# The first image's sampling table, written in whole 2 KB entries from tiles that hold four rows of a column

## The chip, the cores and the metric

The kernel runs on one core of a Trainium2 chip. The metric is the device time of one execution in microseconds (us); for a set of runs the median is given. A core has five engines that run their own instruction streams: PE (TensorE, matrix products and transposes), DVE (VectorE), ACT (ScalarE), POOL (GpSimd) and SP (SyncE, which in this kernel only issues DMAs). [...] A packet is one contiguous run that one DMA engine moves. PE writes its results to PSUM, and DVE or ACT copy them on.

## The reference

The input x is four images of 256 channels and 64 x 64 positions, in float32. Layer 0 adds to x a modulated deformable convolution of the group-normalised image (32 groups): a 3x3 convolution gives, for each position and each of nine taps, an offset in y, an offset in x and a mask; each tap samples the normalised image bilinearly at its displaced position (zero outside the image), is multiplied by the mask, and the nine samples are contracted with w_conv.

```python
om = conv(gn(x), w_off) + b_off                       # 27 channels: 18 offsets, 9 masks
ys = off[:, :, 0] + hs + ki ;  xs = off[:, :, 1] + ws + kj
sampled = bilinear(gn(x), ys, xs) * sigmoid(mask)     # four neighbours with weights
x = x + einsum('bckhw,ock->bohw', sampled, w_conv)
```

Layer 1 treats the 4096 positions of an image as tokens: a layer norm, an attention over the four images with eight heads, a second layer norm, and a mixture of eight experts of which each token takes two. Nothing of layer 1 is touched here.

## The kernel before

**The table.** Bilinear sampling is done by fetching rows. For each image the kernel writes a table to HBM (`tables[b]`, line 327) of 66 x 67 entries, one for each position with a border. An entry is 2 KB: the 256 channels of the position one row above (the half `two=0`), and then the 256 channels of the position itself (`two=1`). Entry (y, x) thus holds the image's rows y-1 and y, counted from zero, at column x-1. One indirect DMA on POOL (line 748, `gather`) then fetches for 128 positions and one tap two adjacent entries, 4 KB in a row, which are the four neighbours. There are 1152 gathers, 288 for an image.

**The first image.** Images 1 to 3 are prepared among the sampling steps of the image before them; image 0 has nothing to hide under, and its preparation is the head of the kernel:

1. SP loads image 0 (4 MB) in four pieces of 1 MB: a half of the channels, and a half of the 4096 positions each (`load_piece`, lines 360 to 370). Behind them on SP's queue come w_off in two DMAs (line 376), b_off (382), w_conv in two of 1.1 MB (394) and the router (168).
2. SP writes the zero borders of the table (`borders`, lines 404 to 408; five DMAs of 64 to 260 KB). The one of line 406 writes the 134 half entries of the table's last row.
3. DVE takes the group statistics: sixteen `bn_stats` of 512 positions (line 446), each as soon as its piece is there, then a short chain over PE and POOL.
4. In eight blocks of eight image rows, DVE normalises (line 508), PE transposes 128 positions at a time (`turn`, line 517), and ACT and DVE copy the result to a tile `zt` (`leave`, line 530), in which a partition holds one position at a time. For image 0 the eight tiles `zt` are the buffers `gs[0..7]`, into which the gathers will write later. With two rows of 64 positions to a transpose, partitions 0 to 63 of `zt` hold the even rows of the block and partitions 64 to 127 the odd ones, four of them behind each other.
5. After each block SP stores it to the table with four DMAs (line 536): one for each half of the partitions (`yl`) and each half of the entry (`two`). Each moves 256 KB from 64 partitions, in 256 packets of 1 KB, to every second row of the table.
6. PE, ACT and DVE compute offsets, indices and weights of the first two blocks (`offsets`, `positions`). Then the sampling steps start: the gathers, four weighted sums of corners (ACT line 765, DVE line 774), a transpose, and the products with w_conv.

**What sets the order.** For image 0 the order on DVE, ACT and PE is written out: the list `first`, sorted by numbers of steps, is emitted as it stands (lines 711 to 725). The order on SP is the framework's, and it is that of the program. The framework also gives the DMAs of SP's queue eight completion semaphores in turn, and the compiled instruction list shows each DMA waiting until the one eight places before it on the queue has landed. The first gather (line 748) waits for all DMAs that write the table and for the indices of block 0; the gathers then wait for free buffers.

Of the kernel before, what the change touches and what calls it, by code (L numbers as in the profile page):

```python
# [18 lines left out]
B, C, H, W = 4, 256, 64, 64  # L19
HW = H * W  # L20
NCH = C // P
# [6 lines left out]
TH, TW = H + 2, W + 3  # L28
# [9 lines left out]
RB = BLK // W  # L38
# [64 lines left out]
def conv_attn_moe_kernel(  # L103
# [22 lines left out]
    nc = tc.nc  # L126
# [200 lines left out]
    tables = [dram.tile([TH * TW, 2 * C], F32, name=f"table{b}") for b in range(B)]  # L327
# [5 lines left out]
    with ExitStack() as actx:  # L333
# [23 lines left out]
        def image_tile(b):  # L357
            xraw[b] = axs[b % 2].tile([P, NCH, HW], F32, name=f"xraw{b}", tag="xraw")

        def load_piece(b, n):  # L360
            ch, h = divmod(n, 2)
            cols = slice(h * HW // 2, (h + 1) * HW // 2)
            return nc.sync.dma_start(
                xraw[b][:, ch, cols],
                x[b, ch * P : (ch + 1) * P].rearrange("p h w -> p (h w)")[:, cols],
            )

        image_tile(0)
        for n in range(2 * NCH):
            load_piece(0, n)  # L370


        woff_sb = aw.tile([P, NCH, 3, 3, QUAD], F32, name="woff_sb")
# [10 lines left out]
        for kj in range(3):  # L384
            ps = slice(kj * QUAD, (kj + 1) * QUAD)
# [11 lines left out]

        zeros = aw.tile([P, C], F32, name="zeros")
        G.memset(zeros, 0.0)

        def borders(b):
            tv = tables[b].rearrange("(y x) (two c) -> y x two c", x=TW, two=2)
# [15 lines left out]
        for half in range(2):  # L418
            ps = slice(half * 64, half * 64 + 64)
# [9 lines left out]
        params, stores = {}, {}  # L429

        def pieces(b):
# [31 lines left out]
            n = FIRST  # L463
            out_ = later if b else first
            for ch in range(NCH):
                for j in range(NBLK):
                    at = LOADS[2 * ch + 2 * j // NBLK] + LANDED + j % (NBLK // 2)
# [13 lines left out]
            tv = tables[b].rearrange("(y x) (two c) -> y x two c", x=TW, two=2)  # L481
            oms = []

            def block(q, at, table=True, offsets=True, alone=False):

                out_ = [] if alone else later
                y0 = q * RB - 1
                lo, hi = max(y0, 0), min(y0 + RB + 2, H)
                if not offsets:
                    lo, hi = y0 + 1, y0 + RB + 1  # L490
                t = {}
                between = "" if table else "_"

                def norm(ch):
                    if ch == 0:
                        t["xs"] = apad.tile(
                            [P, NCH, RB + 2, W], F32, name=f"xs{b}_{q}{between}",
                            tag="xs" if table or alone else "xs_",
                            bufs=2 if table or alone else 1,
                        )  # L500
                        if offsets and lo > y0:
                            G.memset(t["xs"][:, :, 0, :], 0.0)
                        if offsets and hi < y0 + RB + 2:
                            G.memset(t["xs"][:, :, RB + 1, :], 0.0)
                    to, of = t["xs"][:, ch, lo - y0 : hi - y0], xrv[:, ch, lo:hi]
                    scale, bias = rs[:, ch : ch + 1], nb[:, ch : ch + 1]
                    if alone:
                        V.tensor_scalar(to, of, scale, bias, ALU.mult, ALU.add)
                    else:
                        S.activation(to, of, AF.Identity, bias=bias, scale=scale)  # L510


                def turn(i):
                    xc = t["xs"][:, :, 1 : RB + 1].rearrange("p ch y x -> p ch (y x)")
                    t["tp"] = ps_tp.tile([P, C], F32, name=f"tpx{b}_{q}_{i}", tag="tp")
                    for ch in range(NCH):
                        T.transpose(
                            t["tp"][:, ch * P : (ch + 1) * P], xc[:, ch, i * P : (i + 1) * P],
                            ident,
                        )  # L520

                def leave(i):
                    if i == 0:

                        t["zt"] = (
                            gs[q].rearrange("p (t c) -> p t c", c=C) if alone
                            else azt.tile([P, NT, C], F32, name=f"zt{b}_{q}", tag="zt")
                        )
                    zt = t["zt"]
                    (V.tensor_copy if alone and i == NT - 1 else S.copy)(zt[:, i, :], t["tp"])  # L530
                    if i < NT - 1:
                        return
                    for yl in range(2):
                        for two in range(2):
                            yy = q * RB + yl + 1 - two
                            stores[b] = nc.sync.dma_start(
                                tv[yy : yy + RB - 1 : 2, 1 : W + 1, two, :].rearrange(
                                    "t x c -> x t c"
                                ),
                                zt[yl * W : (yl + 1) * W],  # L540
                            )


                def rows_of(n):
                    if n == 0:
                        t["po"] = ps_om.tile([3 * QUAD, RB, W], F32, name=f"po{b}_{q}", tag="om")
                    ch, ki = divmod(n, 3)
                    T.matmul(
                        t["po"], woff_sb[:, ch, ki].rearrange("p kj o -> p (kj o)"),
                        t["xs"][:, ch, ki : ki + RB],  # L550
                        start=(n == 0), stop=(n == NCH * 3 - 1),
                    )

                oc = ocs[q % 2 if table else 2]

                def shifted(kj):
                    ps = slice(kj * QUAD, (kj + 1) * QUAD)
                    to = slice(max(0, 1 - kj), W - max(0, kj - 1))
                    of = slice(max(0, kj - 1), W - max(0, 1 - kj))
                    S.activation(  # L560
                        oc[ps, :, to], t["po"][ps, :, of], AF.Identity, bias=boff_sb[ps]
                    )

                def summed(half):
                    if half == 0:
                        t["pt"] = ps_om.tile([P, NT, NOFF], F32, name=f"pt{b}_{q}", tag="om")
                    ocf = oc.rearrange("p y x -> p (y x)")
                    for i in range(half * 2, half * 2 + 2):
                        T.matmul(
                            t["pt"][:, i, :], ocf[:, i * P : (i + 1) * P], tap_sum,  # L570
                            start=True, stop=True,
                        )

                def kept():
                    if b and not q:
                        oms.append(atmp.tile([P, NR, NOFF], F32, name=f"om{b}", tag="om"))
                    of[q] = oms[0][:, rows_in(q), :] if b else atmp.tile(
                        [P, NT, NOFF], F32, name=f"om{b}_{q}", tag="om_", bufs=2
                    )
                    V.tensor_copy(of[q], t["pt"])  # L580

                out_.append((at, lambda: norm(0)))
                out_.append((at + 1, lambda: norm(1)))
                if alone and table:
                    for i in range(NT):
                        out_.append((at + 10 + 2 * i, lambda i=i: turn(i)))
                        out_.append((at + 11 + 2 * i, lambda i=i: leave(i)))
                elif table:
                    for i in range(NT):
                        out_.append((at + 3 + 4 * i, lambda i=i: turn(i)))  # L590
                        out_.append((at + 4 + 4 * i, lambda i=i: leave(i)))
                if offsets:
                    for m in range(NCH * 3):
                        out_.append((at + 4 + 2 * m + m // 2, lambda m=m: rows_of(m)))
                    for kj in range(3):
                        out_.append((at + 18 + kj, lambda kj=kj: shifted(kj)))
                    out_.append((at + 22, lambda: summed(0)))
                    out_.append((at + 23, lambda: summed(1)))
                    out_.append((at + 24, kept))
                return out_  # L600

            of = {}

            def rows_in(q):
                return slice(q * NT, (q + 1) * NT)
# [85 lines left out]
            if b:  # L691
# [5 lines left out]
                half = NR // 2  # L697
# [13 lines left out]
            for q in range(NBLK):  # L711
                first.extend(block(q, n + 10 * q, offsets=False, alone=True))
            n += 10 * NBLK + 8
            for q in range(EARLY):
                at = n + 20 * q
                first.extend(block(q, at, table=False, alone=True))
                first.extend(positions(rows_in(q), lambda q=q: of[q], at + 25, 4))
            for q in range(EARLY, NBLK):
                at = (q - 2) * NT * K2 + 12
# [234 lines left out]
        with tc.manual_schedule(engines=order):  # L954
# [7 lines left out]
            for n in range(total + TAP + OUT + 3 * NT):  # L962
                b, at = divmod(n, STEPS)
# [43 lines left out]
    for b in range(B):  # L1007
        for j in range(NBLK):
            if j < HB:
                n = j * B + b  # L1010
# [38 lines left out]
    with ExitStack() as bctx:  # L1049
# [130 lines left out]
        rows = NCH * B  # L1180
# [972 lines left out]
```

## Time and profile before

| what | value |
|---|---|
| median of four runs | 3334.86 us (3330.86 to 3343.88) |
| the profiled execution's own time | 3316.29 us |
| its span, from the first to the last instruction | 3314.5 us |
| busy share of PE, DVE, ACT, POOL | 88%, 74%, 57%, 53% |
| bytes moved, mean rate | 913.00 MB, 275 GB/s |
| table stores of image 0 (line 536) | 32 DMAs of 256 KB, issued from 24.0 to 58.6 us |
| first gather starts | 63.59 us |

The profile is of one execution. Its times count from the first instruction; its own time is 1.8 us longer than its span, which lies around the instructions. A group of instructions is named by its line in the kernel, its engine, the operation, and what it writes from what it reads. On SP's queue the length shown for a DMA is the time for which the queue was occupied with issuing it, waiting included, and not the time of the transfer. The waits name the last thing an instruction waited for, as far as the profile can tell.

### The profile page before, as it was taken

What the parts mean: (1) busy time and instruction counts of PE and PEld (TensorE: products, weight loads), DVE (VectorE), ACT (ScalarE), POOL (GpSimd) and SP (SyncE); (2) the same over time, 40 slices, a digit from 0 to 9 for tenths busy, and PEclk for the clock granted to TensorE, in tenths of its full rate; (3) what the DMA queues carried; (4) which work ended last, traced back from release to release, by engine and by line L of the source; (5) the groups of instructions that cost most, each with busy time, mean ns of one, the idle gap of its engine ahead of it and who ended that gap; (6) DMA issues with size and microseconds to landing.
All of it is one profiled execution on the core that took longest, in us unless ns stands there. A gap on an engine that the chain in (4) does not pass through costs nothing. (4 is left out here: it accounts for less than half of the span.)

```text
span 3314.5 us, 45522 instructions
## 1 busy us (share of the span) xinstructions
PE 2911.6 (88%) x11356; PEld 1700.2 (51%) x11356; DVE 2465.4 (74%) x6413; ACT 1887.0 (57%) x4462; POOL 1749.6 (53%) x1809
## 2 busy tenths in 40 slices
PE   4899998898988899988999999997768788889997
PEld 2445544354444444434444444554434477778885
DVE  5878888987878978888889877885546574434776
ACT  2557665565655566645666656756534455546675
POOL 2555566665656655556666633215553466564442
PEclk7999999999999999999999999998888899999998
DMA  8999999999999999999999969614334445545988
GB/s 270 368 320 351 336 368 368 393 362 341 379 356 370 371 351 353 368 336 378 358 356 362 353 163 177 119 56 145 122 129 136 131 141 163 165 134 173 337 289 274
DMA packets 348547, 913.00 MB, mean 275 GB/s; under 512 B 42566, under 2 KB 125821, under 8 KB 345984
## 3 DMA queue, kind: packets, MB, share of 16 engines
q0 software_dynamic: 208368, 689.10, 58.2%
q1 hardware_dynamic: 129488, 197.93, 19.4%
q10 hardware_dynamic: 10432, 23.07, 1.8%
q8 instruction: 95, 1.56, 0.2%
q14 instruction: 164, 1.34, 0.1%
HBM read 741.09 MB, written 171.60 MB: 275 GB/s over the span
## 5 line engine op out<-in xcount | busy, mean ns | idle before, releaser
L748 POOL DMA_INDIRECT g<-table,idx x1152 | 1107.0, 961 | 765.5 <-DVE s L774 383.2
L808 PE MATMUL acc<-sT,wconv_sb 128*128 128x512 f32 x2304 | 1221.9, 613 | 26.1 <-ACT sT L796 11.1
L774 DVE SCALAR_TENSOR_TENSOR partial<-g,wts,s 128x256 f32<-128x256 f32 x1152 | 565.5, 491 | 233.2 <-ACT s L765 114.0
L765 ACT ACTIVATE s<-g,wts 128x256 f32<-128x256 f32 x1152 | 589.2, 511 | 196.1 <-DMA g<-table,idx 110.9
L788 PEld LDWEIGHTS tps<-ident,s 128*128 128x128 f32 x2304 | 304.5, 149 | 718.9 <-issue 481.1
L796 ACT COPY sT<-tps 128x256 f32<-128x256 f32 x1152 | 422.1, 366 | 401.3 <-PE tps L788 134.1
L788 PE MATMUL tps<-ident,s 128*128 128x128 f32 x2304 | 467.7, 286 | 141.6 <-issue 57.0
L774 DVE SCALAR_TENSOR_TENSOR s<-g,wts,s 128x256 f32<-128x256 f32 x1152 | 551.2, 478 | 0.0
L774 DVE SCALAR_TENSOR_TENSOR s<-g,wts,partial 128x256 f32<-128x256 f32 x1152 | 546.4, 474 | 0.7
L1935 POOL DMA_INDIRECT ys_rows<-y,to x277 | 275.5, 995 | 289.8 <-DVE y L1930 215.1
L808 PEld LDWEIGHTS acc<-sT,wconv_sb 128*128 128x128 f32 x2304 | 358.9, 196 | 38.6 <-issue 15.4
L1907 PE MATMUL ph<-xT,w 128*128 128x256 f32 (+1 forms) x1288 | 281.6, 362 | 52.3 <-ACT hT L1911 26.7
L1508 POOL DMA_INDIRECT xs_rows<-u,slots x256 | 248.3, 970 | 114.9 <-issue 69.0
L1930 DVE TENSOR_TENSOR y<-py,w 128x512 f32<-128x512 f32 (+1 forms) x161 | 99.3, 617 | 238.8 <-PE py L1925 76.6
L1925 PE MATMUL py<-w,hT 128*128 128x256 f32 x1108 | 273.2, 387 | 0.6 <-ACT w L1874 0.6
L1907 PEld LDWEIGHTS ph<-xT,w 128*128 128x128 f32 x1288 | 215.3, 195 | 82.5 <-ACT hT L1911 36.5
L1911 ACT ACTIVATE hT<-ph,w 128x256 f32<-128x256 f32 (+1 forms) x322 | 134.9, 443 | 198.3 <-PE ph L1907 95.7
L1925 PEld LDWEIGHTS py<-w,hT 128*128 128x128 f32 x1108 | 212.4, 195 | 30.0 <-ACT w L1874 1.0
L1290 DVE SCALAR_TENSOR_TENSOR mix<-pv,att,mix 128x512 f32<-128x512 f32 x192 | 132.8, 743 | 88.4 <-remote 78.1
L1325 PE MATMUL po<-wo_sb,mix 128*128 128x265 f32 x512 | 135.2, 419 | 37.3 <-DVE mix L1314 36.0
L322 DVE SCALAR_TENSOR_TENSOR junk<-q,k 128x512 f32<-128x512 f32 x224 | 141.5, 686 | 21.0 <-ACT k L1107 21.0
L1299 ACT ACTIVATE gate<-pg,bg_c 128x512 f32<-128x512 f32 x60 | 40.2, 683 | 202.4 <-DVE mix L1314 129.7
(291 smaller groups left out, 3599.1 us busy)
## 6 DMA issues: line engine op xcount, KB each, us to landing
xt<-xs_rows SPq DMA_DIRECT2D x116, 260.0 KB
yk<-ys_rows SPq DMA_DIRECT2D x56, 512.0 KB
table<-zt SPq DMA_DIRECT2D x96, 256.0 KB
g<-table,idx POOLq DMA_INDIRECT x1152
t<-o SPq DMA_DIRECT2D x32, 530.0 KB
t<-bo_sb POOLq DMA_DIRECT2D x32, 530.0 KB
dt<-t SPq DMA_DIRECT2D x64, 265.0 KB
xraw<-in_x SPq DMA_DIRECT2D x16, 1024.0 KB
```

What stands on the lines that cost most here:

```text
L322: V.scalar_tensor_tensor(junk, qks[s_, j, ch][0], 1.0, qks[t_, j, ch][1], ALU.mult, ALU.mult, accum_out=parts[:, ch, s_ * B + t_, j : j + 1],)
L748: g = G.indirect_dma_start(out=gs[n % NGB], out_offset=None, in_=tables[b], in_offset=bass.IndirectOffsetOnAxis(ap=params[b][0][:, r, k : ...
L765: first = S.activation(ss[n], gs[n % NGB][:, :C], AF.Copy, scale=params[b][1][:, 0, r, k : k + 1])
L774: last_corner[n] = V.scalar_tensor_tensor(kept if c == 1 else ss[n], gs[n % NGB][:, c * C : (c + 1) * C], params[b][1][:, c, r, k : k + 1] ...
L788: T.transpose(tps[n][:, ch * P : (ch + 1) * P], s[:, ch * P : (ch + 1) * P], ident)
L796: S.copy(sTs[tap][:, :, i * P : (i + 1) * P], tps.pop(n).rearrange("p (ch t) -> p ch t", ch=NCH),)
L808: T.matmul(accs[block, oh], wconv_sb[:, ch, k, oh * P : (oh + 1) * P], sTs[tap][:, ch, :], start=(k == 0 and ch == 0), stop=(k == K2 - 1 a ...
L1325: T.matmul(po[:, n, :CR], o[:, ch, i * P : (i + 1) * P], wo_sb[:, ch, :], start=(ch == 0), stop=(ch == NCH - 1),)
L1508: s = G.indirect_dma_start(out=rows_, out_offset=bass.IndirectOffsetOnAxis(ap=slots[:, k, n : n + 1], axis=0), in_=u[:, n % NT, :], in_off ...
L1907: T.matmul(ph, w1_sb[:, ch, f * P : (f + 1) * P], xT[:, ch, :], start=(ch == 0), stop=(ch == NCH - 1),)
L1925: T.matmul(py[:, i, :], hT[:, f, i * P : (i + 1) * P], w2_sb[:, f, :], start=(f == 0), stop=(f == NCH - 1),)
L1935: s = G.indirect_dma_start(out=ys_rows[g], out_offset=bass.IndirectOffsetOnAxis(ap=to[:, i : i + 1], axis=0), in_=y[:, i, :], in_offset=No ...
```

## The change

Two things change, both for image 0 only. The line numbers of the changed kernel are up to 24 higher from there on.

First, image 0 is loaded in eight pieces of 512 KB (a half of the channels, a quarter of the positions) where there were four of 1 MB.

Second, the rows of a block are dealt out otherwise, and the table is stored otherwise. DVE's normalisation writes the eight rows in the order 0, 4, 1, 5, 2, 6, 3, 7, by an access pattern alone, so that the transposes put rows 0 to 3 of the block on partitions 0 to 63 and rows 4 to 7 on partitions 64 to 127. A partition of `zt` then holds four consecutive rows of one column, one behind the other, and two neighbouring kilobytes in it are a whole table entry. `leave_whole` stores each half of the partitions with three DMAs: three whole entries of each column (192 packets of 2 KB, read from overlapping windows of the tile, 384 KB), the first half of the entry behind them and the second half of the entry ahead of them (64 packets of 1 KB each, 64 KB). That is six DMAs for a block where there were four, 48 where there were 32, and the same 8 MB.

```diff
-        def load_piece(b, n):
-            ch, h = divmod(n, 2)
-            cols = slice(h * HW // 2, (h + 1) * HW // 2)
+        def load_piece(b, n, each=2):
+            ch, h = divmod(n, each)
+            cols = slice(h * HW // each, (h + 1) * HW // each)
...
-        for n in range(2 * NCH):
-            load_piece(0, n)
+        for n in range(4 * NCH):
+            load_piece(0, n, 4)
...
+        def overlapping(rows, n):
+
+            at = rows.ap
+            return bass.AP(rows.tensor, rows.offset, [at[0], [C, n], [1, 2 * C]])
...
                     if alone:
+                        if table:
+
+                            to = to.rearrange("p (m h) w -> p m h w", h=2)
+                            of = of.rearrange("p (h m) w -> p m h w", h=2)
                         V.tensor_scalar(to, of, scale, bias, ALU.mult, ALU.add)
...
                     if i < NT - 1:
                         return
+                    if alone:
+                        leave_whole(zt)
+                        return
...
+                def leave_whole(zt):
+
+                    half = RB // 2
+                    th = tables[b].rearrange("(y x) e -> x y e", x=TW)
+                    for h in range(2):
+                        ps, r = slice(h * W, (h + 1) * W), q * RB + h * half
+                        nc.sync.dma_start(
+                            th[1 : W + 1, r + 1 : r + half], overlapping(zt[ps], half - 1)
+                        )
+                        nc.sync.dma_start(tv[r + half, 1 : W + 1, 0], zt[ps, half - 1])
+                        stores[b] = nc.sync.dma_start(tv[r, 1 : W + 1, 1], zt[ps, 0])
```

The four stores of a block (line 536) stay for images 1 to 3, and so do their loads in four pieces.

## The prediction

> **What bounds the kernel now.** The change touches the first 64 us, so I read the profile from there. First, busy times by stretch (columns: stretch, length, busy us of PE, PEld, DVE, ACT and POOL, PE's granted clock, share and rate of the DMA engines):
>
> ```profile
> 0.00:24.00 24.00, 3.87 (x16) 3.37 (x16) 16.49 (x39) 2.44 (x5) 7.18 (x21) 1.00 0.85 297
> 24.00:62.00 38.00, 23.74 (x94) 12.78 (x92) 16.02 (x57) 12.64 (x30) 0.21 (x1) 0.83 0.87 230
> 62.00:68.00 6.00, 0.00 (x0) 0.00 (x0) 0.00 (x0) 0.05 (x1) 3.50 (x4) 0.50 0.49 116
> 68.00:168.00 100.00, 80.34 (x273) 38.39 (x274) 88.15 (x220) 53.84 (x130) 62.41 (x66) 0.87 0.98 372
> ```
>
> The head has two halves. To 24 us the DMA engines load and DVE computes statistics; from 24 to 62 us they are 87% busy, at only 230 GB/s, while every compute engine is mostly idle. From 68 us on they are 98% busy with gathers, so what the head loses nothing wins back, and what it saves moves the end one for one.
>
> Second, the timeline of SP's queue, and of the engines it serves (columns: start, us, engine, line, what):
>
> ```profile
> 16.34 0.80 SPq L406 DMA_DIRECT2D table<-zeros  x1
> 17.19 5.15 SPq L407 DMA_DIRECT2D table<-zeros  x1
> 22.38 0.79 SPq L408 DMA_DIRECT2D table<-zeros  x1
> 24.03 35.64 SPq L536 DMA_DIRECT2D table<-g  x32
> ```
>
> ```profile
> 33.22 0.42 DVE L530 COPY g<-tpx 128x256 f32<-128x256 f32 x1 [0.99 <-PE tpx L517]
> ...
> 56.43 0.19 DVE L643 TENSOR_TENSOR wts<-lo 128x36 f32<-128x36 f32 x1
> ```
>
> ```profile
> 63.59 1.24 POOL L748 DMA_INDIRECT g<-table,idx  x1 [31.55 <-DMA bo_c<-in_bo]
> ...
> 67.95 0.51 ACT L765 ACTIVATE s<-g,wts 128x256 f32<-128x256 f32 x1 [13.97 <-DMA g<-table,idx]
> 68.49 0.49 DVE L774 SCALAR_TENSOR_TENSOR partial<-g,wts,s 128x256 f32<-128x256 f32 x1 [11.86 <-ACT s L765]
> ```
>
> DVE normalises from 20.68 us, the first tile is complete at 23.96, the last at 33.64, and the last weights of the two prepared blocks at 56.6. The 32 stores occupy SP from 24.03 to 59.67, 1.11 us each. The completion events of the trace put the last landing at 62.6 (2.9 us after its issue ended), POOL starts the first gather 0.95 later, and its data reach ACT at 67.95 and DVE at 68.49. So the table's stores end last; the compute chain has 68.49 - 56.62 = 11.9 us to spare.
>
> Third, what a store costs SP (columns: ns least/median/most), and what the DMA engines reach from 26 to 61 us (the stores) and from 3304 to 3306 us (output, 2 KB packets from 128 partitions):
>
> ```profile
> L536 SPq DMA_DIRECT2D table<-g x32: 574/1132/1893, 24.0 to 58.6; - x32
> ...
> L404 SPq DMA_DIRECT2D table<-zeros x4: 677/786/1216, 14.8 to 1391.1; - x4
> ...
> L405 SPq DMA_DIRECT2D table<-zeros x4: 595/646/730, 15.7 to 1391.8; - x4
> ...
> L2023 ACTq DMA_DIRECT2D out<-oT x27: 383/384/452, 3062.3 to 3288.4; - x27
> ```
>
> ```profile
> DMA packets 8450, 8.17 MB, mean 233 GB/s; under 512 B 496, under 2 KB 8448, under 8 KB 8448
> ...
> DMA packets 375, 0.74 MB, mean 368 GB/s; under 512 B 18, under 2 KB 18, under 8 KB 375
> ```
>
> SP is held back while it issues the stores: an unhindered one takes 0.57, the median 1.13. The limit is behind it, at 233 GB/s. The packet records say more: between 26 and 61 us half of the 1 KB packets took 44 to 48 ns and three in eight 65 to 85, with little between, while of the 1 KB packets from 200 to 1700 us, spread between gathers, 96% took 46 or 47. A 1 KB packet is not slow in itself; something is shared in the head that is shared by bytes. What the head has and those have not is sixteen DMA engines reading the same 64 partitions at once.
>
> **The change part by part.**
>
> *Image in eight pieces.* The first `bn_stats` starts at 5.99, when 1 MB has landed. At 424 GB/s (the same view for 4 to 12 us) 512 KB less is 1.2 us. DVE then runs gapless to 17.25 (16 statistics of 0.61 us and 1.5 us of small work), and later pieces come every 1.24 us for 1.22 us of work, so the first tile is complete at about 22.8. But SP issues the last border (line 408) until 23.2, because line 407 was held 5.15 us: the 134 rows of line 406 go through one DMA engine (one completion event, at 27.8). That does not move, so the first store starts at about 23.4: -0.6 us. The four further issues (0.4 us each) push w_off on SP from 3.0 to about 4.6 us; and since the pieces now take all eight completion semaphores, w_off and w_conv each wait for a piece of the image. Their packets stand behind the image anyway: w_off landed at 15.2 and is read at 34.2, w_conv at 21.7, read at 80.8. Cost nothing; without that cover, 1.6 us.
>
> *Row order.* Sixteen DVE instructions of 0.49 us with another pattern, runs of 64 elements. Bounds: nothing, or 0.04 each (the 0.53 of the 576-element form), 0.6 us, under the stores, as tiles are complete 26 us before the last store. Nothing.
>
> *Stores, DMA side.* The 8.39 MB stay. If bytes over shared partitions are the limit, 8.39 MB / 233 GB/s = 36.0 us, as before, 2.23 us for each of sixteen half blocks (35.64 / 16). If packets were the limit, the nearest row is the output, 368 GB/s: 22.8 us, 1.43 each. That row has 2 KB packets and also 128 partitions; the stores get only the first. The two heaps decide: I take 2.23.
>
> [...]
>
> *Stores, SP side.* A half block was two issues and is now three. The whole one (192 packets) is nearest to the unhindered line 536, 0.60. The small one has its twins in lines 404 and 405, the same shape into the same table: 0.60 to 0.85 in the head; I take 0.62. With 0.05 between issues: 0.60 + 2 x 0.62 + 0.15 = 1.99 us, 31.8 for sixteen. Bounds: 0.38 for a small one (the output's issue) gives 1.49 and 23.8 us; 0.79 (median of line 404) gives 2.36 with 0.63 for the whole, 37.8 us.
>
> *Semaphores.* A DMA waits for the one eight places ahead. That was 2 MB of stores and is 1.33 MB, 5.7 us of work against 2.9 us from issue to landing: enough. The sixth store still waits for line 406 (27.8); it would be ready at 26.5. Until then five stores with 0.98 MB are out, 4.2 us of transfer from 24 on: the engines do not run dry. Behind a blocked SP stand only further stores, and the small vectors of line 157 that come in 60 us too early.
>
> *Sum.* The half block costs the larger of 2.23 (DMA) and 1.99 (SP). Start -0.6; the stretch 0, or -1 where SP's deeper queue lets the two partition halves overlap more; I take -1. First gather at 62.0 instead of 63.59: **-1.6 us**, from 3316.3 to 3314.7 for the profiled execution. The median shown lies 18.6 us above that, so 3333.3. Outer bounds: with 1.49 for a half block the stores are done before the weights, which come 1.2 us earlier too, and the spare ends at 12 to 13 us: -12.6. With 2.36, 37.8 - 35.6 - 0.6 = +1.6.
>
> **The rivals.**
>
> *A, SP becomes the bound at 1.99.* If 2 KB packets pass faster, the stores take 31.8 instead of 35.64, start 0.6 earlier, and the last small one lands some 1.7 us sooner after its issue: -6 us, 3329. For it: 84 ns for a 2 KB packet in the output. Against it: the two heaps. Still within 0.3%.
>
> *B, both limits give way.* Small issues at 0.38 and packets at the output's rate: -10 to -12.6 us, 3322 to 3325. Against it: no 64-row store of this trace was issued in under 0.57.
>
> *C, slower: SP's issue takes the place of the transfer.* 48 issues instead of 32, at the place where SP stands before every store. It decides once a small store takes over 0.74 us (0.60 + 2 x 0.74 + 0.15 = 2.23). One of the two twins in the head took 0.85: 2.45 each, 39.2 us, +3 us after the earlier start, 3338. For it: the median of line 404. Against it: line 405 in the same place, 0.60.
>
> *D, no change at all,* since the border of line 406 and the bytes both stay: 0, 3335.
>
> **How the numbers follow.** Forecast (0 to -3 us) 0.5, A 0.2, B 0.08, C 0.12, D 0.1. A measurement of this kernel tells some 0.3% (10 us) from no change; the four runs shown span 13 us. Only B crosses that line by itself, and a noisy comparison adds a few in a hundred on either side: faster 0.11, same 0.82, slower 0.07. The range takes in B's near end at the bottom (3325) and C with the runs' spread at the top (3341).
>
> **What would show it.** Right: line 536's successors occupy SP until 57 to 59 us at about 230 to 245 GB/s, whole stores held above 0.6 us; the first gather at 61 to 63; `bn_stats` from 4.8 us with no earlier first store to match than 23.2. Wrong: first gather before 56, rate over 300 GB/s in the stretch (2 KB packets did pass faster, or both halves of the partitions are read together); or small stores of 0.8 us and a gather after 64; or a difference that arises behind 68 us.

## The result, and the profile after

The changed kernel takes 3342.89 us (median of 52 runs, 3330.09 to 3360.09), the kernel before 3331.03 us (78 runs, 3311.17 to 3345.80). The ratio is **1.0037, 95% interval [1.0028, 1.0046]**: slower by 12 us, with an interval of 9.3 to 15.3 us. The prediction was 1.6 us less than before, 3333.3 us in a range of 3324 to 3341. It started from the median of the four runs shown to it, 3334.86, which lies 3.8 us above that of all 78.

The profiled execution of the changed kernel took 3353.99 us (span 3352.2). Its timeline, SP's queue from the last borders to the fourth store, then two half blocks of the steady part (start, us, engine, line; line 561 is the whole store of 384 KB, 564 and 565 the two small ones of 64 KB):

```profile
17.84 5.47 SPq L412 DMA_DIRECT2D table<-zeros  x1
23.37 0.38 SPq L413 DMA_DIRECT2D table<-zeros  x1
23.86 0.88 SPq L561 DMA_DIRECT2D table<-g  x1
24.78 1.36 SPq L564 DMA_DIRECT2D table<-g  x1
26.18 2.19 SPq L565 DMA_DIRECT2D table<-g  x1
28.41 1.26 SPq L561 DMA_DIRECT2D table<-g  x1
...
39.96 0.61 SPq L561 DMA_DIRECT2D table<-g  x1
40.61 0.62 SPq L564 DMA_DIRECT2D table<-g  x1
41.27 1.34 SPq L565 DMA_DIRECT2D table<-g  x1
42.72 0.60 SPq L561 DMA_DIRECT2D table<-g  x1
43.37 0.62 SPq L564 DMA_DIRECT2D table<-g  x1
44.02 1.33 SPq L565 DMA_DIRECT2D table<-g  x1
```

The first store starts 0.17 us earlier than before (23.86 for 24.03). From then on SP repeats one figure: 0.60, 0.62, and a third issue of 1.34 that is held. A half block takes some 2.72 us (2.68 and 2.76 in turn), where it took 2.23, and the last store's issue ends at 69.87 instead of 59.67. What comes behind it, on the timeline of POOL, ACT and DVE:

```profile
55.62 0.19 DVE L667 TENSOR_TENSOR wts<-lo 128x36 f32<-128x36 f32 x1
...
72.70 1.24 POOL L772 DMA_INDIRECT g<-table,idx  x1 [41.00 <-DMA beta_c<-in_beta]
...
77.14 0.51 ACT L789 ACTIVATE s<-g,wts 128x256 f32<-128x256 f32 x1 [23.97 <-DMA g<-table,idx]
...
77.68 0.49 DVE L798 SCALAR_TENSOR_TENSOR partial<-g,wts,s 128x256 f32<-128x256 f32 x1 [21.86 <-ACT s L789]
```

The weights are ready 0.8 us earlier than before, and the first gather starts 9.1 us later (72.70 for 63.59); ACT and DVE follow 9.2 us late. (The profile puts POOL's wait down to the DMA of a small vector, beta_c, that happened to land just then; the last store had landed at 71.57, 1.1 us before the gather, against 1.0 us before the change.) The 9.2 us lie just under the median's 9.3 to 15.3; whether a few us more arise later, two single profiles cannot tell. The stretches (length, busy us of PE, PEld, DVE, ACT, POOL, PE's granted clock, share and rate of the DMA engines) show where it lies:

```profile
0.00:24.00 24.00, 4.56 (x19) 4.05 (x20) 17.29 (x40) 3.09 (x6) 7.18 (x21) 1.00 0.86 292
24.00:74.00 50.00, 22.97 (x91) 12.09 (x89) 15.41 (x56) 12.25 (x29) 1.44 (x2) 0.76 0.80 178
32.00:69.00 37.00, 15.10 (x44) 6.42 (x44) 8.32 (x39) 6.59 (x12) 0.00 (x0) 0.74 0.87 193
74.00:174.00 100.00, 76.51 (x260) 36.05 (x261) 84.82 (x212) 52.12 (x128) 61.72 (x64) 0.87 0.97 367
```

From 32 to 69 us the DMA engines are as busy as they were (0.87), but move 193 GB/s where they moved 233. The engines, no idler than before, take longer for the same bytes: the packet records of this stretch give 149 ns on average for a 2 KB packet and 68 for one of 1 KB. Before, 1 KB took 61 on average and some 48 at the median, and the output's 2 KB packets took 84.

### The profile page after: what moved, and what is told of

Read it like the earlier page. It is cut to its first block, busy times and chain, and to the rows that moved or that the text cites. A ratio compares the mean times of both kernels' runs of the same rounds, so it can differ in the third digit from the quotient of the medians.

```text
span 3352.2 us, 45545 instructions
## 1 busy us (share of the span) xinstructions
PE 2926.8 (87%) x11356; PEld 1715.3 (51%) x11356; DVE 2465.6 (74%) x6413; ACT 1883.1 (56%) x4462; POOL 1750.0 (52%) x1809
## 5 line engine op out<-in xcount | busy, mean ns | idle before, releaser
L1931 PE MATMUL ph<-xT,w 128*128 128x256 f32 (+1 forms) x1288 | 288.8, 370 | 50.7 <-ACT hT L1935 24.4
L1931 PEld LDWEIGHTS ph<-xT,w 128*128 128x128 f32 x1288 | 222.1, 201 | 80.3 <-ACT hT L1935 31.5
```

Of the source, the lines that this page charges most:

```text
L1931: T.matmul(ph, w1_sb[:, ch, f * P : (f + 1) * P], xT[:, ch, :], start=(ch == 0), stop=(ch == NCH - 1),)
```

## The experiments

A half block moves 512 KB, for each of the 16 DMA engines (a store of the table leaves 16 landing events) either 32 packets of 1 KB, or 12 of 2 KB and 8 of 1 KB. So the packet times split its period into packet time and idle time: after, 12 x 149 + 8 x 68 = 2.33 us of packets and, at a share of 0.87, 0.35 of idling; before, 32 x 61 = 1.95 and 0.27. The loss is 0.38 us in the packets and 0.08 in idling. Three theories for the packets: **S**, sixteen engines that read one half of the 128 partitions share the reading of it, and in the changed kernel they do so all the time; **W**, 2 KB packets out of overlapping windows are slow in themselves; **I**, three issues instead of two. The kernels ran on two further chips, on which the kernel before takes 3372.8 (the first four experiments) and 3378.9 us (the others); each ratio is against it on the same chip.

**1. The changed kernel, rows on even and odd partitions.** The same 48 stores, but the upper four rows of a block lie on the even partitions and the lower four on the odd ones, so that each store reads partitions from the whole width.

```diff
-                            to = to.rearrange("p (m h) w -> p m h w", h=2)
+                            to = to.rearrange("p r w -> p (r w)").rearrange(
+                                "p (m w h) -> p m h w", w=W, h=2
+                            )
...
-                        ps, r = slice(h * W, (h + 1) * W), q * RB + h * half
+                        ps, r = slice(h, P, 2), q * RB + h * half
```

> The changed kernel, with one difference: the two groups of four rows are dealt to even and odd partitions instead of the lower and the upper 64, so that every store reads 64 partitions spread over all 128. Number, size and order of the DMAs and the places they write stay. Theory S (sixteen DMA engines share the reading of one half of the partitions, in step): a 2 KB packet falls from 150 to about 84 ns and a 1 KB packet to 46; the half block falls from 2.70 us to SP's own 1.95 to 2.0, the first gather from 72.7 to 57 to 59, the time by 14 us against the changed kernel and by 4 to 6 against the one before. Theory W (the 2 KB packets are slow by the way they read overlapping windows or write rows that lie 137 KB apart): packets stay at 150 ns, the half block at 2.70, the first gather at 72 to 73. Theory I (three issues instead of two are what costs): also no change, 72 to 73.

Ratio 0.9983 [0.9967, 0.9999], 0.3 to 11 us faster. The timeline, SP's queue and the first gather:

```profile
40.08 0.60 SPq L563 DMA_DIRECT2D table<-g  x1
40.73 0.61 SPq L566 DMA_DIRECT2D table<-g  x1
41.38 0.60 SPq L567 DMA_DIRECT2D table<-g  x1
42.09 0.61 SPq L563 DMA_DIRECT2D table<-g  x1
...
61.05 1.24 POOL L774 DMA_INDIRECT g<-table,idx  x1 [29.62 <-DMA beta_c<-in_beta]
```

The third issue is not held any more; a half block takes 2.0 us, three unheld issues, and the packets take 84 ns (2 KB) and 46 (1 KB). The sizes, the windows and the number of issues are those of the changed kernel, so W falls: a 2 KB packet out of such a window takes 84 ns as soon as the 64 partitions are others. I falls as the cause of the slow packets, since the issues are still three. It is S. The steady pace is the expected one, three unheld issues, but the first two half blocks take 6.0 us (24.21 to 30.20), and so the first gather, at 61.05, is later than the 57 to 59 expected.

What the sixteen engines share, and how the partitions are divided for it, no record shows. An estimate from the packet times, with all sixteen engines at work: a whole store of the changed kernel reaches 16 x 2048 B / 149 ns = 220 GB/s while it runs, one of this run 16 x 2048 B / 84 ns = 390 GB/s.

**2. The kernel before, rows on even and odd partitions.** The old four stores of a block, read in the same way.

```diff
+                            to = to.rearrange("p r w -> p (r w)").rearrange(
+                                "p (m w h) -> p m h w", w=W, h=2
+                            )
+                            of = of.rearrange("p (m h) w -> p m h w", h=2)
...
-                                zt[yl * W : (yl + 1) * W],
+                                zt[yl : P : 2] if alone else zt[yl * W : (yl + 1) * W],
```

> The kernel before, with one difference: the even and odd rows of a block are dealt to even and odd partitions, so that each of its four stores reads 64 partitions spread over all 128; 1 KB packets, 32 stores and 2 x 2 MB loads in four pieces as before. Theory S: the 1 KB packets are all at 46 to 50 ns (half of them were), SP issues the stores at 0.62 to 0.75 us each instead of 1.11, they are out by 46 to 48 us and the first gather starts at 49 to 51; then the weights, ready at 56.6, set the first corner on DVE, 11 to 12 us earlier than 68.5: about 3319, -0.35%. Theories W and I: nothing changes, first gather at 63 to 64.

Ratio **0.9973 [0.9954, 0.9992]**: this version beats the kernel before, and with it the changed one. The stores take 25.3 us instead of 35.6, a packet 48 ns on average, and the rate is 327 GB/s (28 to 49 us). The table's group, and the timeline at the first gather:

```profile
L541 SPq DMA_DIRECT2D table<-g x32: 579/704/1390, 24.1 to 48.7; - x32
```

```profile
53.13 1.24 POOL L753 DMA_INDIRECT g<-table,idx  x1 [21.16 <-DMA bo_c<-in_bo]
...
57.53 0.51 ACT L770 ACTIVATE s<-g,wts 128x256 f32<-128x256 f32 x1 [2.27 <-DMA g<-table,idx]
...
57.99 0.19 DVE L648 TENSOR_TENSOR wts<-lo 128x36 f32<-128x36 f32 x1
58.10 0.49 DVE L779 SCALAR_TENSOR_TENSOR partial<-g,wts,s 128x256 f32<-128x256 f32 x1
```

The first gather comes 10.5 us earlier than before, later than the 49 to 51 expected, and DVE's first corner now directly follows the last weights. The compute chain has caught up with the table, as the outer bound of the prediction's sum had it for faster stores: ACT's first corner, still released by the gather's data, ends at 58.04, and the last weights at 58.18.

**3. The changed kernel's layout with four stores of 1 KB packets.** Load and tiles as changed, but each half of the partitions is stored in two DMAs of 256 KB.

```diff
-                        nc.sync.dma_start(
-                            th[1 : W + 1, r + 1 : r + half], overlapping(zt[ps], half - 1)
-                        )
-                        nc.sync.dma_start(tv[r + half, 1 : W + 1, 0], zt[ps, half - 1])
-                        stores[b] = nc.sync.dma_start(tv[r, 1 : W + 1, 1], zt[ps, 0])
+                        for two in range(2):
+                            yy = r + 1 - two
+                            stores[b] = nc.sync.dma_start(
+                                tv[yy : yy + half, 1 : W + 1, two].rearrange("t x c -> x t c"),
+                                zt[ps],
+                            )
```

> The changed kernel's load and its layout (four rows of a column on a partition, lower and upper 64 partitions), but stored in four DMAs of 256 KB with 1 KB packets for a block, as before the change. Theory S, with SP running only about two DMAs ahead: the two transfers ahead are 512 KB again, the DMA engines do not run dry and can drift apart, the half block is back at 2.1 to 2.3 us, first gather 61 to 64, time within 0.1% of the kernel before. Theory W in the form that the rows' places in HBM are the cause: half block 2.6 to 2.7, first gather 71 to 73. Theory W in the form that the 2 KB windows are the cause, and theory I: as S, 61 to 64.

Ratio 0.9999 [0.9981, 1.0017]; first gather at 64.59.

```profile
L563 SPq DMA_DIRECT2D table<-g x32: 574/1150/1942, 24.4 to 59.6; - x32
```

That is the old store (574/1132/1893) at the old pace, 36.2 us for 35.6, with packets of 59 ns. The new order of the rows costs nothing; what costs is the way the tiles are stored, in a large store of 2 KB packets and two small ones. Experiments 4 and 5 take these two apart.

**4. All whole stores first.** The sixteen whole stores are issued as the tiles come, the 32 small ones behind the last tile.

```diff
-                        nc.sync.dma_start(tv[r + half, 1 : W + 1, 0], zt[ps, half - 1])
-                        stores[b] = nc.sync.dma_start(tv[r, 1 : W + 1, 1], zt[ps, 0])
+                        small.append((tv[r + half, 1 : W + 1, 0], zt[ps, half - 1]))
+                        small.append((tv[r, 1 : W + 1, 1], zt[ps, 0]))
+                    if q == NBLK - 1:
+                        for to, of_ in small:
+                            stores[b] = nc.sync.dma_start(to, of_)
```

> The changed kernel, but the 32 small stores are put off until all 16 whole ones are out, so that each kind is measured alone. Theory S: the whole ones, 12 packets of 150 ns on each engine, come at 1.8 to 1.9 us each, and the small ones at SP's 0.62 to 0.68 each, where the transfer takes 0.3; 16 x 1.85 + 32 x 0.65 = 50 us from about 24, first gather near 77. Theory W: the same for the whole ones. Theory I: whole ones at 0.65 once their tiles are there (36 us), small ones at 0.98 (what two of them take now, 1.95), first gather near 70.

One execution, 3371.31 us, first gather at 73.31. SP's queue:

```profile
24.25 24.02 SPq L562 DMA_DIRECT2D table<-g  x16
...
48.31 22.38 SPq L569 DMA_DIRECT2D table<-g  x32
```

The whole stores take 1.50 us each, not the 1.85 expected. With always another large store behind them, the 2 KB packets take 117 ns on average instead of 149, though out of the same half of the partitions. They fall into two heaps, as the 1 KB packets did before: between 28 and 48 us half of them took 65 to 95 ns, as in experiment 1, and 44% 120 or more, where in the changed kernel 96% took 120 or more. So the packets are not slow because of the half alone: it matters what the sixteen engines do beside each other. (In this run the half also changes with every store, each 384 KB instead of each 512.) The small stores then take 0.70 each, mostly SP's own issue (0.595 at the median, and 0.05 between). The completion records fit. In the changed kernel the sixteen engines finish a store within 0.29 us of each other (median, 33 to 58 us), in the kernel before within 0.77, in experiment 3 within 0.80, and in this run's whole stores within 1.8. In experiment 1 they are closer still, 0.18, and fast, 84 ns: in these runs being in step went with slow packets only where all sixteen read one half (149 ns). That engines which have drifted apart read different halves at the seams between two stores, and engines in step always meet, is the reading of these numbers; no record shows the sharing itself. Why they are in step was the next question.

**5. Two issues for a half block.** Theory D: SP's third store is let in only when the large one two places ahead is nearly through (in the steady part its issue ends 0.8 us before that one's first landing). At that moment only two small stores, 0.55 us of transfer (8 packets of 68 ns for each engine), are left to cover the next issue. The engines run dry at each whole store and start it together. The packet records show the dry moments: in the changed kernel some 14 packets are under way at a time, but between 32 and 69 us there are eleven moments with fewer than 9 (mean over 0.1 us), at the seam before a whole store, as at 41.2 and 43.9. The two small stores are joined into one of 128 KB:

```diff
+        def two_ends(rows, apart):
+            at = rows.ap
+            return bass.AP(rows.tensor, rows.offset, [at[0], [apart, 2], [1, C]])
...
-                        nc.sync.dma_start(tv[r + half, 1 : W + 1, 0], zt[ps, half - 1])
-                        stores[b] = nc.sync.dma_start(tv[r, 1 : W + 1, 1], zt[ps, 0])
+                        stores[b] = nc.sync.dma_start(
+                            two_ends(tv[r, 1 : W + 1, 1], half * TW * 2 * C - C),
+                            two_ends(zt[ps, 0], (half - 1) * C),
+                        )
```

> The changed kernel, with the two small stores of a half block joined into one DMA of 128 KB (128 packets of 1 KB): two issues for a half block instead of three, the same packets into the same places, still out of one half of the partitions. The changed kernel needed 2.70 us for a half block. Theory D (the engines run dry: SP's third store is let in only when the second before it has been read, and the two small ones, 0.55 us of transfer, do not cover the issue of the next whole one): a joined small store has 8 packets of some 68 ns for each engine, 0.55 us in one piece, about as long as an issue; the dry time of 0.2 to 0.3 us at each whole store goes, and the half block takes 2.3 to 2.45, 37 to 39 us for sixteen; the first gather starts at 67 to 69, where the changed kernel's started at 72.7. Theory I (it is the number of issues, by SP's own time): 2.70 - 0.62 = 2.1 us, held by the transfer at 2.23 as in the kernel before; the first gather at 64 to 65. Theory W (2 KB packets out of overlapping windows are slow in themselves, 150 ns, whatever stands beside them): 2.60 or more, the first gather at 71 or later.

Ratio 0.9994 [0.9977, 1.0012]; first gather at 67.05. SP's queue, the group of the large stores, and a line of SP's waits:

```profile
23.91 0.94 SPq L565 DMA_DIRECT2D table<-g  x1
29.04 0.58 SPq L568 DMA_DIRECT2D table<-g  x1
...
40.19 1.43 SPq L565 DMA_DIRECT2D table<-g  x1
41.66 0.62 SPq L568 DMA_DIRECT2D table<-g  x1
42.33 1.66 SPq L565 DMA_DIRECT2D table<-g  x1
44.03 0.62 SPq L568 DMA_DIRECT2D table<-g  x1
```

```profile
L565 SPq DMA_DIRECT2D table<-g x16: 599/1469/1816, 23.9 to 60.6; - x16
```

```profile
SPq L568 <- DMA table<-zeros: 4.1, 1, 4.1
```

The same packets into the same places now take 2.27 us for a half block (31.04 to 60.56 us, 13 of them), as D said, a little better even, and the rate is 229 GB/s. What D had wrong is how the gain divides: idling falls only by 0.15 us for a half block (0.35 to 0.20), while the packets themselves become faster, 122 and 76 ns, 2.07 us for a half block instead of 2.33. The engines now land within 0.58 us of each other, and of the dry moments one is left (31 to 60 us). By the reading above, the dry moment costs more by what it does to the engines' step than by its own length. Theory I, which gave 2.1 and the transfer's 2.23, is near it in time, but not its cause: three unheld issues take 2.0 us (experiment 1), so SP had time left in the changed kernel. The first gather at 67.05 lies in D's range partly by chance, since the joined store has a wait of its own at the start, 4.1 us for the borders, which the large store before it covers only in part. Against the 2.23 of the kernel before, 2.27 is nearly no loss.

**6. The new stores with the image in four pieces.**

```diff
-        for n in range(4 * NCH):
-            load_piece(0, n, 4)
+        for n in range(2 * NCH):
+            load_piece(0, n)
```

> The changed kernel with image 0 in four pieces as before: the new stores alone. If the stores are the whole cause, their period stays at 2.70 us for a half block, the first store starts at about 24.0 instead of 23.86, the weights of the convolution land some 1 us earlier, and the first gather starts at 72 to 73; the ratio to the kernel before stays at 1.002 to 1.005. If the eight pieces carry a part (semaphores taken, w_off and w_conv held), the first gather comes 1 us or more earlier than 72.

Ratio 1.0012 [0.9989, 1.0036], which holds 1 as well as the lower part of the loss. The timeline decides:

```profile
41.19 0.60 SPq L561 DMA_DIRECT2D table<-g  x1
41.83 0.61 SPq L564 DMA_DIRECT2D table<-g  x1
42.48 1.35 SPq L565 DMA_DIRECT2D table<-g  x1
43.88 0.60 SPq L561 DMA_DIRECT2D table<-g  x1
```

The same figure at the same period, 2.7 us, and the first gather at 71.14. The new stores alone carry 7.5 of the 9.1 us; the first gather comes 1.6 us earlier than with eight pieces, a little short of the 1 us below 72 that was set for it, so the pieces seem to carry a part (the profiles of the kernels before and changed are of another chip than this run and the next).

**7. The kernel before with the image in eight pieces,** the same loop the other way round.

> The kernel before with image 0 in eight pieces: the other half of the change alone. The prediction gave it -0.6 us (first store at 23.4, first gather at 63.0). By the changed kernel's trace the first store gains only 0.2 and the border of line 406 lands some 0.7 to 1 us later, which the sixth store waits for: first gather at 63.5 to 64.6, ratio 0.999 to 1.001. If the pieces are a cause of the loss, the first gather starts after 65.

Ratio 1.0007 [0.9990, 1.0025]; first gather at 64.72, 1.1 us later than before instead of 0.6 earlier, just above the 63.5 to 64.6 expected. SP's queue:

```profile
18.59 5.32 SPq L407 DMA_DIRECT2D table<-zeros  x1
23.96 0.38 SPq L408 DMA_DIRECT2D table<-zeros  x1
24.45 36.01 SPq L536 DMA_DIRECT2D table<-g  x32
```

The stores' stretch is the old one (36.0), only later: the border of line 407 is issued 1.4 us later than in the kernel before (18.59 for 17.19). The chip does not explain it: in the six runs with eight pieces this border is issued at 17.84 to 18.59, in the three with four at 16.86 to 17.32. The two halves of the change roughly add up: 7.5 + 1.1 = 8.6 of the 9.1 us.

| kernel | stores on SP, us | 2 KB, 1 KB packet, ns | half block, us | first gather | ratio |
|---|---|---|---|---|---|
| before | 24.0 to 59.7 | -, 61 | 2.23 | 63.59 | 1 |
| changed | 23.9 to 69.9 | 149, 68 | 2.72 | 72.70 | 1.0037 |
| 1 changed, even and odd | 24.2 to 58.6 | 84, 46 | 2.03 | 61.05 | 0.9983 |
| 2 before, even and odd | 24.1 to 49.4 | -, 48 | 1.58 | 53.13 | 0.9973 |
| 3 layout, 1 KB packets | 24.4 to 60.6 | -, 59 | 2.26 | 64.59 | 0.9999 |
| 4 whole stores first | 24.3 to 70.7 | 117, 63 | - | 73.31 | - |
| 5 two issues | 23.9 to 62.7 | 122, 76 | 2.27 | 67.05 | 0.9994 |
| 6 new stores, four pieces | 23.9 to 68.4 | 150, 68 | 2.71 | 71.14 | 1.0012 |
| 7 old stores, eight pieces | 24.4 to 60.5 | -, 59 | 2.25 | 64.72 | 1.0007 |

The half block is that of the steady part for the changed kernel and experiments 1, 5 and 6, and a sixteenth of the whole stretch for the others. Packet times are means.

## Why the prediction was wrong

**The head sets the end one for one: it fits.** The first gather moved by 9.1 us, ACT and DVE by 9.2, the median by 9.3 to 15.3, so up to some 6 us behind the head are not excluded. In experiments 1 to 3 and 5 to 7 the shift of the first gather lies within the interval of the ratio.

**Stores, DMA side: the cause right, the number wrong.** The two heaps of packet times were rightly put down to engines that read one half of the partitions at once: with the 64 partitions spread over all 128, a 2 KB packet fell from 149 to 84 ns (experiment 1) and a 1 KB packet from 61 to 48 (experiment 2). But the step took 2.23 us for a half block as what this limit costs, and 2.23 was an average over engines half in conflict: about half of the packets at 44 to 48 ns, three in eight at 65 to 85. How many conflict depends, by the reading of experiments 4 and 5, on how far the engines have drifted apart, and this the change moved. With nearly all packets in conflict the half block has 2.33 us of packets, where the kernel before had 1.95. The period of 2.72 has the idling besides.

**The failed step is the sum's "the stretch 0, or -1 where SP's deeper queue lets the two partition halves overlap more; I take -1".** That the two halves overlap at all was the author's estimate, and no run shows it. The stretch was +10.4 on SP's queue (23.86 to 69.87, 46.0 us for 35.6): 7.8 in the steady pace, sixteen times 0.49, and the rest at its start, where issues are held up to 2.19; 1.1 came back behind it, as the last store, a small one, lands sooner (first gather 2.8 us after its issue, 3.9 before). The deeper queue did the contrary of what the step hoped: more DMAs on SP's queue were not more bytes ready, since behind a large store there were two small ones, 128 KB, where there had been another of 256.

**"Enough", and "the engines do not run dry": wrong in its place.** The eight semaphores were indeed enough, no steady store waits for one. But SP is held in front of the third store by something else, which the profile shows as an issue of 1.34 us; that it is the transfer two places ahead is read from the landings (0.8 us apart in the steady part) and not tested by itself. The prediction had the sign of it in its own row: line 536's median of 1.13 for an unhindered 0.57 said that SP was already held behind its own earlier stores. (The 5.7 us there should be 6.0, 1.4 MB at 233 GB/s; nothing hangs on it.)

**Stores, SP side: right.** Unheld, the whole store took 0.60 and the small one 0.61 to 0.62, against 0.60 and 0.62; 1.99 us for three showed as 2.03 in experiment 1, where nothing else held them. Rivals A and C hung on this. A's pace came true once the 64 partitions were spread (2.03 us), but not its -6 us (first gather at 61.05, 2.5 earlier than before, with eight pieces that cost 1.1); C had the right sign for a wrong reason, since no small store of the steady part cost over 0.74 by itself. (The lower bound is 0.60 + 2 x 0.38 + 0.15 = 1.51, 24.2 us for sixteen, and not 1.49 and 23.8.)

**Image in eight pieces: -0.6 predicted, +1.1 measured (experiment 7).** DVE did start earlier, 5.00 for 5.99, and normalises at 19.98 for 20.68. But the step's "that does not move" for the borders fell. The image landed at 14.42 instead of 13.63, and w_off's second DMA, on which SP is held in both kernels, let the queue go at 11.19 instead of 10.40. So the borders came 0.6 to 1.0 us later (that of line 407, 412 after, at 17.84 for 17.19), the border of line 406 (411 after), which goes through one DMA engine alone (it leaves one landing event, a piece of the image sixteen), landed at 28.6 instead of 27.7, and w_conv at 23.0 instead of 21.6. The first store found its tile ready and SP busy. "Cost nothing" counted only the readers of w_off and w_conv and not what stands behind them on SP's queue.

**Row order nothing: right** (experiment 3 against 7: 64.59 and 64.72).

The chances followed from the cases, and none of them held a mechanism by which the stores' transfer itself becomes slower: C's 0.12 stood for SP alone. The upper bound of 37.8 us for sixteen half blocks was taken from issue times. The bound from the DMA side was there to be worked out: all packets in the second heap, at its middle of 75 ns, are 32 x 75 = 2.40 us for a half block, at the share of 0.87 2.76, and 44 us for sixteen; 16 x 2.72 = 43.5 is what the steady pace came to.

## What to carry to other kernels

The same 2 KB packets from the same 64 partitions took 117, 122 or 149 ns here, by what stood in the queue with them: before carrying a transfer's mean to another order of the same bytes, look at the distribution of its packets, and bound the new order by the case in which all of them conflict. Two small DMAs behind a large one on the same queue cost more than their bytes here: the engines ran low at the seam before a large store (eleven moments with fewer than 9 packets under way between 32 and 69 us), and with the two joined a half block took 2.27 us instead of 2.72, where the kernel before took 2.23. Where 64 rows of a tile are stored at a time, laying them on every second partition (by the writing engine's access pattern alone: DVE's normalisation took 0.543 us for 512 elements on each partition, and 0.541 before) took 35.6 us of stores down to 25.3 (experiment 2).

## What the runs showed of the hardware that was not expected

- The same 2 KB packets from the same 64 neighbouring partitions take 149, 122 or 117 ns, by what else stands in the queue; from 64 alternate partitions, 84.
- Loading 4 MB in pieces of 512 KB instead of 1 MB delivered the first piece 1 us earlier (4.98 for 5.96) and the whole 0.8 us later.
- Where stores read one half of the partitions, the spread of the landings of a store's sixteen shares went with the conflict: 0.29 us apart at 149 ns for 2 KB, 0.58 at 122, 1.8 at 117; in the old form of 1 KB packets 0.77 to 0.80 at 59 to 61. From alternate partitions it did not: 0.18 apart at 84 ns.
